# A state space block with its order on PE, DVE and ACT fixed by the program text, and its preparation cut into more steps

## The chip, the cores and the metric

The kernel runs on one core of one Trainium2 chip. Its time is device microseconds for one execution, as the median of several runs. A profile of one further execution gives every instruction with its engine, its start and its length. The engines are named as the profile names them: PE (TensorE's matmuls), PEld (its weight loads), DVE (VectorE), ACT (ScalarE), POOL (GpSimd) and SP (SyncE, which issues the DMAs here).

## The reference

Two layers, each of an attention-like block and a feed-forward block with residuals: attention, a mixture of 32 experts with top 8, a state space block, and a gated feed-forward whose weights are looked up in a table of 16 values. All arrays are f32; there are 2 sequences of 1024 tokens, and the model's width is 512. The change lies in the third block and in the beginning of the fourth:

```python
def _L1_attn_ref(x, w_in, w_param, w_out):        # 16 heads, D_STATE = D_HEAD = CHUNK = 64
    xr = x @ w_in.T
    inp, res = (xr[..., :D_INNER], xr[..., D_INNER:])
    params = (x @ w_param.T).reshape(b, l, N_HEADS, PARAM_DIM)
    dt = jax.nn.softplus(params[..., 0])
    a = jnp.exp(-dt)
    Bp = params[..., 1:1 + D_STATE]
    Cp = params[..., 1 + D_STATE:]
    y = _ssd(a.reshape(nb, l), ...)                # heads and tokens reshaped flat: nb = b * heads
    out = y.reshape(b, l, D_INNER) * jax.nn.silu(res)
    return out @ w_out.T

def _ssd(a, Bm, Cm, X, Q):
    cs = jnp.cumsum(jnp.log(a).reshape(nb, nc, Q), axis=-1)
    L = jnp.where(tri, jnp.exp(cs[..., :, None] - cs[..., None, :]), 0.0)
    y_diag = einsum('znij,znjh->znih', einsum('znid,znjd->znij', Cc, Bc) * L, Xc)
    states = einsum('znj,znjd,znjh->zndh', jnp.exp(cs[..., -1:] - cs), Bc, Xc)
    # scan over chunks: S = exp(cs[..., -1]) * S + states
    y_inter = einsum('znid,zndh,zni->znih', Cc, S_prev, jnp.exp(cs))
    return (y_diag + y_inter).reshape(nb, l, dh)

x = x + _L1_attn_ref(_layernorm(x), ...)
x = x + _L1_ffn_ref(_layernorm(x), ...)            # h = silu(gate(x)) * up(x); down(h)
```

## The kernel before

The kernel computes the four blocks in turn. For the attention and the expert blocks the order of the instructions on PE, DVE and ACT is that of the program text (`tc.manual_schedule`); SP's and POOL's order is a planner's. For the state space block (`_state_space`) and the final feed-forward (`_FeedForward`) a planner, which has priorities from the program's order and its own estimate of each instruction's time, orders all engines ahead of the launch. On the chip each engine then takes its instructions strictly in that order, and waits where an operand or a buffer isn't ready.

The state space block takes 128 tokens of each of the two sequences at a time: a stage `st`, eight in all. Each stage has eight chunks `c`, and `k = 8 st + c` counts them.

- `prepare(st)` loads the residual rows `x` and the experts' sums `part`, adds them (L1370) and takes their moments (L1372, L1373), the root and the reciprocal (L1375, L1376); normalises and turns the rows (L1381, L1387, L1388); multiplies by the step weights (`dt`, L1393), sends `dt` through HBM into another layout (L1400, L1403), takes the softplus by Exp and Ln (L1410, L1411), and sums it with a triangular matrix (`la`, `laT`, `cs`: L1423 to L1431); the sums go to HBM as `cs_rows` (L1433). It is a generator, with four `yield`s.
- `features(st)` makes B, C, X and the gate for a stage: 32 groups of matmuls into one of two PSUM banks (`pf`, L1443). A group of the first 24 is copied out by four copies, ACT and DVE in turn (L1460, L1462); a group of the last eight (the gate) by one copy (L1469 or L1471). Every group ends with a `yield`.
- `begin(k)` loads the rows `csb` by two DMAs (L1484), turns B and X for the chunk (`bx`, L1489 to L1492), makes the decays (`dec`, L1495 on DVE, Exp at L1499 on ACT), `xd` and `cd` on POOL, and `ec` (Exp, L1513).
- `weights(k)` multiplies C by B (`cb`, L1529) and by the decay (`wgt`, L1535). `products(k)` makes the state (L1547, L1579), the output (`ps_y`, L1557, L1569), and multiplies it into the gate (L1592).
- `project_out(st)` multiplies a stage's output by `wout` (`so`, L1598), adds it to `x` (L1603) and stores it in `x3` (L1605), in two halves.

The main loop (L1619) interleaves them: while stage `st` runs its chunks, the features of `st + 1`, the output of `st - 1` and the preparation of `st + 2` are given out between them by `step`. In the last stage there are no features; the final feed-forward's first tokens are normalised and its first units run there (`_FeedForward.begin`, L1698; `unit`, L1681). PSUM's eight banks are two for features (`ps_f`), two for turns and projections (`ps_t`), and one each for `st`, `y`, `cb0` and `cb1`.

Ahead of the loop two preparations and the features of stage 0 are written one after the other:

```python
        for st in range(2):
            for _ in prepare(st):
                pass
        for _ in features(0):
            pass
        begun = begin(0)
        wgt = weights(0, begun[1])
```

## Time and profile before

Three runs took 2804.3, 2810.66 and 2813.29 us; the median is 2810.66. The profiled execution took 2820.1 us, of which 2818.4 lie between its first and last instruction.

| | PE | PEld | DVE | ACT | POOL |
|---|---|---|---|---|---|
| busy in the whole span, us | 2703.1 | 1624.1 | 1425.4 | 933.1 | 635.7 |
| share | 96% | 58% | 51% | 33% | 23% |

The mean granted TensorE clock is 0.982 of full speed. The state space block runs from about 1550 us to 2403 us: the loads of its first rows wait for the experts' last scattered sums until 1556 us, its first matmul runs at 1566.8, the Silu of the gate, which opens a stage, runs at 1646.96, 1730.91, 1827.97, 1925.09, 2022.16, 2119.21, 2216.39 and 2307.49, and the last output projection ends at 2396.5. Of DVE's 50.1 us in a middle stage (1825.9 to 1923.0), 15.8 copy features out, 10.3 make the decays and 9.2 the gate products. In the block the loads are light: the DMA engines are busy for a sixth of the time in a middle stage.

A line of a profile view shows the source line, the engine, the operation, the tile written and the tiles read (out<-in), shapes and counts. In the order of time a line begins with start and length in us, and ends in brackets with the idle time of the engine before it and who ended it. In the table by stretches, each line has its borders and length, and then the busy time of each engine with its number of instructions, the granted clock, the share of the DMA engines and GB/s.

### The profile page before, as it was taken

What the parts mean: (1) busy time and instruction counts of PE and PEld (TensorE: products, weight loads), DVE (VectorE), ACT (ScalarE), POOL (GpSimd) and SP (SyncE); (2) the same over time, 40 slices, a digit from 0 to 9 for tenths busy, and PEclk for the clock granted to TensorE, in tenths of its full rate; (3) what the DMA queues carried; (4) which work ended last, traced back from release to release, by engine and by line L of the source; (5) the groups of instructions that cost most, each with busy time, mean ns of one, the idle gap of its engine ahead of it and who ended that gap; (6) DMA issues with size and microseconds to landing.
All of it is one profiled execution on the core that took longest, in us unless ns stands there. A gap on an engine that the chain in (4) does not pass through costs nothing. (4 is left out here: it accounts for less than half of the span.)

```text
span 2818.4 us, 34644 instructions
## 1 busy us (share of the span) xinstructions
PE 2703.1 (96%) x11976; PEld 1624.1 (58%) x11976; DVE 1425.4 (51%) x3952; ACT 933.1 (33%) x1887; POOL 635.7 (23%) x787
## 2 busy tenths in 40 slices
PE   7999999998989899999999699999999999999999
PEld 3444444544465566666665587777777775444444
DVE  5555543655236788987775344554455453101100
ACT  1344432443323233333333333443444433101010
POOL 2222220433355634333333000110111010000000
PEclk9999999998989999999999799999999999999999
DMA  3376532212479999998886301111111140100000
GB/s 115 111 199 184 164 115 70 92 60 74 153 247 248 241 228 255 263 240 202 205 205 107 84 16 36 38 41 44 28 47 42 35 147 20 34 8 27 30 0 26
DMA packets 242793, 315.60 MB, mean 112 GB/s; under 512 B 60753, under 2 KB 129361, under 8 KB 241841
## 3 DMA queue, kind: packets, MB, share of 16 engines
q1 hardware_dynamic: 208320, 234.87, 28.0%
q0 software_dynamic: 33280, 77.68, 13.1%
q8 instruction: 98, 1.61, 0.2%
q10 hardware_dynamic: 1008, 0.73, 0.1%
q14 instruction: 87, 0.70, 0.1%
HBM read 160.17 MB, written 153.04 MB: 111 GB/s over the span
## 5 line engine op out<-in xcount | busy, mean ns | idle before, releaser
L1080 PE MATMUL pg<-xgT,wgu 128*128 128x256 f32 (+1 forms) x1536 | 447.2, 444 | 13.8 <-DVE hT L1093 12.7
L1080 PEld LDWEIGHTS pg<-xgT,wgu 128*128 128x128 f32 x1536 | 289.0, 194 | 161.1 <-issue 51.2
L1142 POOL DMA_INDIRECT acc<-y,tok x160 | 272.9, 1706 | 401.8 <-ACT y L1140 186.7
L943 DVE SCALAR_TENSOR_TENSOR acc<-hit,lut,acc 128x688 f32<-128x688 bf16 (+2 forms) x405 | 348.8, 861 | 14.4
L1443 PE MATMUL pf<-xT,win 128*128 128x256 f32 x1024 | 242.5, 385 | 5.5 <-ACT gate L1471 3.8
L653 ACT ACTIVATE pT<-st 128x512 f32<-128x512 f32 (+3 forms) x384 | 158.7, 497 | 180.6 <-PE st L640 158.0
L548 PE MATMUL sp<-ka,qa 64*128 64x512 f32 (+3 forms) x768 | 207.3, 511 | 8.1 <-DVE mx L569 4.0
L1443 PEld LDWEIGHTS pf<-xT,win 128*128 128x128 f32 x1024 | 187.0, 190 | 38.8 <-PE pf L1443 7.2
L640 PE MATMUL st<-qa,ka 64*128 64x512 f32 (+3 forms) x768 | 182.4, 512 | 2.3 <-issue 1.5
L569 DVE TENSOR_REDUCE mx<-sp 128x1 f32<-128x384 f32 (+3 forms) x352 | 167.3, 492 | 17.4 <-PE sp L548 10.7
L657 POOL TENSOR_SCALAR_AFFINE_SELECT pT<-pT 128x128 f32<-128x128 f32 x256 | 83.5, 338 | 390.2 <-ACT pT L653 378.3
L296 POOL DMA_INDIRECT rows<-row,idx x128 | 128.7, 1005 | 108.3 <-DVE chosen L282 43.6
L1750 PE MATMUL po<-wd,f_hT 128*128 128x512 f32 (+1 forms) x352 | 152.6, 592 | 0.0
L671 PE MATMUL y<-pT,v 128*64 128x512 f32 (+3 forms) x768 | 145.7, 512 | 4.6 <-ACT raw L608 3.1
L562 DVE CUSTOM_DVE_ANT_0 junk<-sp,cmask 128x128 f32<-128x128 f32 x256 | 73.3, 286 | 145.3 <-PE sp L548 135.4
L548 PEld LDWEIGHTS sp<-ka,qa 64*128 64x128 f32 x768 | 91.8, 187 | 93.5 <-issue 49.7
L1694 DVE TENSOR_TENSOR f_hT<-s,pu 128x512 f32<-128x512 f32 (+1 forms) x37 | 25.5, 688 | 232.8 <-PE pu L1688 232.8
L640 PEld LDWEIGHTS st<-qa,ka 64*128 64x128 f32 x768 | 102.3, 192 | 63.2 <-issue 36.9
L1515 POOL TENSOR_TENSOR cd<-ft_c,ec 128x256 f32<-128x256 f32 x56 | 40.8, 730 | 413.3 <-PE cb L1529 205.2
L1140 ACT ACTIVATE y<-yo,rw 128x512 f32<-128x512 f32 x128 | 81.2, 684 | 157.9 <-PE yo L1133 150.1
L1443 PE MATMUL pf<-xT,wc 128*128 128x256 f32 x512 | 125.0, 391 | 8.8 <-DVE ft_b L1462 5.2
L1688 PE MATMUL pg<-f_xT,wg 128*128 128x512 f32 (+1 forms) x296 | 133.4, 593 | 0.0
(213 smaller groups left out, 4034.3 us busy)
## 6 DMA issues: line engine op xcount, KB each, us to landing
rows<-blank SPq DMA_DIRECT2D x160, 272.5 KB
xg<-rows SPq DMA_DIRECT2D x32, 817.5 KB
xg<-rows SPq DMA_DIRECT2D x32, 545.0 KB
csb<-cs_rows SPq DMA_DIRECT2D x128, 128.0 KB
wgu<-in_wg_dram SPq DMA_DIRECT2D x32, 256.0 KB
wgu<-in_wu_dram SPq DMA_DIRECT2D x32, 256.0 KB
wd<-in_wd_dram SPq DMA_DIRECT2D x32, 256.0 KB
wd<-in_wd_dram SPq DMA_DIRECT2D x64, 128.0 KB
```

Of the source, the lines that this page charges most:

```text
L296: t = tc.nc.gpsimd.indirect_dma_start(out=self.rows[:, :], out_offset=bass.IndirectOffsetOnAxis(ap=idx[:, i, k : k + 1], axis=0), in_=xr[i ...
L548: nc.tensor.matmul(sp[hh][:, c0:c1], lhsT=q[half, pr, tb * P : (tb + 1) * P], rhs=k[half, pr, k0 * P : k1 * P], start=True, stop=True,)
L569: nc.vector.tensor_reduce(m[:, n : n + 1], sp[hh][:, c0:c1], AX.X, ALU.max)
L640: nc.tensor.matmul(st[:, c0:], lhsT=k[half, j // 2, kb * P : (kb + 1) * P], rhs=q[half, j // 2, qt * 512 + c0 : (qt + 1) * 512], start=Tru ...
L653: e = nc.scalar.activation(pT[:, c0:], st[:, c0:], AF.Exp)
L671: nc.tensor.matmul(y[j // 2][half, c0:], lhsT=v[:, kb, h // 2, h % 2 : h % 2 + 2, :].rearrange("p k d -> p (k d)"), rhs=ps[j][:, c0:], sta ...
L943: nc.vector.scalar_tensor_tensor(acc, hit, lut[:n, k : k + 1], acc, ALU.mult, ALU.add)
L1080: nc.tensor.matmul(pg, lhsT=wgu[:, cc, m * P : (m + 1) * P], rhs=xgT[:, cc, :cols], start=cc == 0, stop=cc == NCC - 1,)
L1142: nc.gpsimd.indirect_dma_start(out=self.router.acc[to][:, :], out_offset=bass.IndirectOffsetOnAxis(ap=tok[:, j : j + 1], axis=0), in_=y, i ...
L1443: nc.tensor.matmul(pf, lhsT=w[wn][:, cc, c0 : c0 + P], rhs=xT[st][:, cc], start=cc == 0, stop=cc == NCC - 1,)
L1688: nc.tensor.matmul(dst[:n, :], lhsT=w[:, cc, fc * P : fc * P + n], rhs=self.xT[tt][:, cc, :], start=cc == 0, stop=cc == NCC - 1,)
L1750: nc.tensor.matmul(po, lhsT=self.hT[tt][fc // 4][:n, fc % 4, j * P : (j + 1) * P], rhs=wd[:n, fc, :], start=fc == 0, stop=fc == NFC - 1,)
```

## The change

The whole of `_state_space` now runs under `tc.manual_schedule` for PE, DVE and ACT: these three take their instructions in the order in which the text gives them out. SP and POOL stay with the planner.

- `prepare` has seven `yield`s where it had four: after its loads, between the moments of its two blocks of rows, and after `dt`'s way through HBM. It begins in chunk 3 (loads), goes on in chunk 4 (two steps: a sum and its moments each, the second with root and reciprocal), chunk 5 (normalise and turn), 6 (`dt`) and 7 (softplus), and its last step (`laT`, `cs`) comes at the start of chunk 2 of the following stage. It was given out in chunks 4 to 7.
- The loads of `csb` are taken out of `begin` and given out by `load` a chunk earlier. `begin` becomes a generator of two parts, and feature groups are given out singly, between them.
- In chunk 0 of each stage, where ACT has the Silu of the gate, all four copies of a feature group go to DVE (`busy`).
- Ahead of the loop, steps of the two preparations are written between the groups of features(0).
- In the last stage the feed-forward's rows are both loaded at once, into two tiles, its moments are taken in a second step and all four blocks turned in a third; a unit is given out in two halves. At the end, units that were begun are finished.

```diff
@@ -1354,7 +1354,9 @@
         def block(st, b):
             return (b * T + st * ST) // P
 
-        xs, xT, cs_rows, csT, gate, ft = {}, {}, {}, {}, {}, {}
+        xs, xT, cs_rows, csT, gate, ft, csbs = {}, {}, {}, {}, {}, {}, {}
+
+        busy = [False]
 
         def prepare(st):
 
@@ -1365,12 +1367,13 @@
                 r = slice(block(st, b) * P, (block(st, b) + 1) * P)
                 nc.sync.dma_start(out=x[:, b, :], in_=acc[0][r, :])
                 nc.sync.dma_start(out=part[:, b, :], in_=acc[1][r, :])
+            yield
             mv = g["small"].tile([P, B, 2], F32, tag="ln_mv", name="ln_mv")
             for b in range(B):
                 nc.vector.tensor_tensor(x[:, b, :], x[:, b, :], part[:, b, :], ALU.add)
-                stats = g["small"].tile([P, 6], F32, tag="ln_st", name="ln_st")
-                nc.vector.bn_stats(stats, x[:, b, :])
-                nc.vector.bn_aggr(mv[:, b, :], stats)
+                _moments(nc, g, x, b, mv[:, b, :])
+                if b == 0:
+                    yield
             rstd = g["small"].tile([P, B], F32, tag="ln_rs", name="ln_rs")
             nc.scalar.activation(rstd, mv[:, :, 1], AF.Sqrt, bias=g["eps"])
             nc.vector.reciprocal(rstd, rstd)
@@ -1403,6 +1406,7 @@
             nc.sync.dma_start(
                 out=d, in_=dt_rows.rearrange("b (n t) h -> (b n) (t h)", t=CT)
             )
+            yield
 
             neg = wk.tile([NROW, P], F32, tag="neg", name="neg", bufs=1)
             nc.vector.tensor_scalar(neg, d, -1.0, None, ALU.mult)
@@ -1456,7 +1460,7 @@
                             src = pf[h2 * HB : (h2 + 1) * HB, b, :].rearrange(
                                 "p (c t) -> p c t", t=CT
                             )
-                            if h2 == 0:
+                            if h2 == 0 and not busy[0]:
                                 nc.scalar.copy(dst, src)
                             else:
                                 nc.vector.tensor_copy(dst, src)
@@ -1475,15 +1479,22 @@
 
             return [(s, b, b * SCH + s * NCH + c) for s in range(NSEQ) for b in range(B)]
 
+        def load(k):
+
+            if k < NST * NCH:
+                st, c = divmod(k, NCH)
+                csb = csbs[k] = wk.tile([P, NSEQ, B, P], F32, tag="csb", name="csb", bufs=3)
+                for s in range(NSEQ):
+                    nc.sync.dma_start(
+                        out=csb[:, s], in_=cs_rows[st][:, s, c, :].partition_broadcast(P)
+                    )
+
         def begin(k):
+
 
             st, c = divmod(k, NCH)
             f = ft[st]
-            csb = wk.tile([P, NSEQ, B, P], F32, tag="csb", name="csb", bufs=3)
-            for s in range(NSEQ):
-                nc.sync.dma_start(
-                    out=csb[:, s], in_=cs_rows[st][:, s, c, :].partition_broadcast(P)
-                )
+            csb = csbs.pop(k)
             pt = ps_t.tile([P, 2, NSEQ, P], F32, tag="t", name="bx_ps")
             for s in range(NSEQ):
                 nc.tensor.transpose(pt[:, 0, s, :], f["b"][:, s * NCH + c, :], g["ident"])
@@ -1497,6 +1508,7 @@
                     ALU.subtract, ALU.min,
                 )
             nc.scalar.activation(dec, dec, AF.Exp)
+            yield
             xd = cd = ec = None
             if c < NCH - 1:
 
@@ -1513,7 +1525,9 @@
                     nc.scalar.activation(ec[half], csb[half, :, b, :], AF.Exp)
                 cd = wk.tile([P, NSEQ, P], F32, tag="cd", name="cd")
                 nc.gpsimd.tensor_tensor(cd, f["c"][:, c :: NCH, :], ec, ALU.mult)
-            return bx, dec, xd, cd, ec
+            made[k] = bx, dec, xd, cd, ec
+
+        made = {}
 
         def weights(k, dec):
 
@@ -1609,44 +1623,63 @@
             for _ in range(n):
                 next(it, None)
 
-        for st in range(2):
-            for _ in prepare(st):
-                pass
-        for _ in features(0):
+
+        first, second, feats = prepare(0), prepare(1), features(0)
+        for of, n in ((first, 1), (second, 1), (first, 3), (feats, 4), (first, 1), (feats, 3),
+                      (second, 1), (feats, 2), (second, 1), (feats, 1), (first, 1), (feats, 4),
+                      (first, 1), (second, 1), (feats, 4), (second, 1), (feats, 5), (second, 1),
+                      (feats, 4), (second, 1), (feats, 6)):
+            step(of, n)
+        load(0)
+        load(1)
+        for _ in begin(0):
             pass
-        begun = begin(0)
-        wgt = weights(0, begun[1])
+        wgt = weights(0, made[0][1])
+        ahead = iter(())
         for st in range(NST):
             lasts = iter(())
             if st == NST - 1:
                 last.weights = then()
                 last.banks = [(ps_f, "f"), (ps_f, "f")]
-                lasts = last.begin(wk, ps_t)
-            nc.scalar.activation(gate[st], gate[st], AF.Silu)
+                lasts = last.begin(wk, xp, ps_t)
             feats = features(st + 1) if st + 1 < NST else iter(())
             out = project_out(st - 1) if st else iter(())
-            ahead = prepare(st + 2) if st + 2 < NST else iter(())
             for c in range(NCH):
                 k = st * NCH + c
                 more = k + 1 < NST * NCH
-                if c < NCH - 1:
-                    nxt = begin(k + 1)
+                nxt = begin(k + 1) if more else iter(())
+                load(k + 2)
+                busy[0] = c == 0
+                if c == 0:
+                    nc.scalar.activation(gate[st], gate[st], AF.Silu)
+                if c == 2:
+                    step(ahead)
+                    ahead = prepare(st + 2) if st + 2 < NST else iter(())
+                if c == 3:
+                    step(ahead)
+                step(feats)
+                if c in (4, 5, 6):
+                    step(ahead)
+                step(nxt)
+                step(lasts, (1, 1, 2, 2, 1, 1, 1, 1)[c])
+                step(feats)
+                step(nxt)
                 if c < 2:
                     step(out)
-                step(lasts, (1, 0, 2, 2, 1, 1, 1, 1)[c])
-                step(feats, 2)
-                if c >= 4:
+                if c in (4, 7):
                     step(ahead)
                 step(feats)
-                if c == NCH - 1 and more:
-                    nxt = begin(k + 1)
-                bx, dec, xd, cd, ec = begun
+                bx, dec, xd, cd, ec = made.pop(k)
                 products(k, bx, xd, cd, ec, wgt)
                 if more:
-                    wgt = weights(k + 1, nxt[1])
-                    begun = nxt
+                    wgt = weights(k + 1, made[k + 1][1])
+                if c > 2:
+                    step(lasts)
                 step(feats)
+                busy[0] = False
         for _ in project_out(NST - 1):
+            step(lasts, 2)
+        while last.begun > last.done:
             step(lasts)
 
 
@@ -1657,6 +1690,7 @@
     def __init__(self, tc, g, x3, out, big):
         self.tc, self.g, self.x3, self.out, self.big = tc, g, x3, out, big
         self.hT, self.xT = {}, {}
+        self.begun = self.done = 0
 
     def rows(self, fc):
         return FTAIL if fc == NFC - 1 else P
@@ -1679,11 +1713,15 @@
         ]
 
     def unit(self, tt, fc, pool, tag):
+
         nc = self.tc.nc
         wg, wu, _ = self.weights
         n = self.rows(fc)
+        self.begun = fc + 1
         p = [q.tile([P, TT], F32, tag=k, name="p" + k) for q, k in self.banks]
-        for dst, w in zip(p, (wg, wu)):
+        for i, (dst, w) in enumerate(zip(p, (wg, wu))):
+            if i:
+                yield
             for cc in range(NCC):
                 nc.tensor.matmul(
                     dst[:n, :], lhsT=w[:, cc, fc * P : fc * P + n], rhs=self.xT[tt][:, cc, :],
@@ -1695,25 +1733,28 @@
             self.hT[tt][fc // 4][:n, fc % 4, :], s[:n, :], p[1][:n, :], ALU.mult
         )
 
-    def begin(self, wk, psum):
+    def begin(self, wk, xp, psum):
 
         nc, g = self.tc.nc, self.g
+        x = [
+            wk.tile([P, B, D], F32, tag="part", name="part", bufs=1),
+            xp.tile([P, B, D], F32, tag="x", name="x", bufs=3),
+        ]
         for i in range(2):
-            x = wk.tile([P, B, D], F32, tag="part", name="part", bufs=1)
-            self.load(x, self.tokens(0)[2 * i : 2 * i + 2])
-            norms = _norms(nc, g, x, range(B))
-            yield
-            if i == 0:
-                self.room(0)
-            nc.vector.reciprocal(norms[1], norms[1])
+            self.load(x[i], self.tokens(0)[2 * i : 2 * i + 2])
+        yield
+        norms = [_norms(nc, g, x[i], range(B)) for i in range(2)]
+        yield
+        self.room(0)
+        for i in range(2):
+            nc.vector.reciprocal(norms[i][1], norms[i][1])
             for b in range(B):
-                xn = _normed(nc, x, b, b, norms, wk, ("xn", D))
+                xn = _normed(nc, x[i], b, b, norms[i], wk, ("xn", D))
                 _turn(nc, g, xn, 2 * i + b, self.xT[0], psum, "t")
             yield
-        self.done = 0
         for fc in range(NFC):
+            yield from self.unit(0, fc, wk, "xn")
             self.done = fc + 1
-            self.unit(0, fc, wk, "xn")
             yield
 
     def rest(self):
@@ -1760,7 +1801,8 @@
             pending = None
             for tt in range(NTT):
                 for fc in range(0 if tt else self.done, NFC):
-                    self.unit(tt, fc, wk, "s")
+                    for _ in self.unit(tt, fc, wk, "s"):
+                        pass
                 if pending is not None:
                     down(*pending)
                 pending = (tt, x)
@@ -1868,7 +1910,10 @@
 
     big = second.enter_context(tc.tile_pool(name="ss_big", bufs=2, reuse_waits="tile"))
     last = _FeedForward(tc, g, x3, out, big)
-    _state_space(tc, g, a, w, acc, x3, last_weights, big, last)
+    with tc.manual_schedule(
+        engines={getattr(mybir.EngineType, n) for n in ("PE", "DVE", "Activation")}
+    ):
+        _state_space(tc, g, a, w, acc, x3, last_weights, big, last)
     last.rest()
     second.close()
 ```

## The prediction

> **What bounds the kernel now.** I read the page's slices first: PE is at nine tenths or more almost everywhere, so the block that changes can only give back the time in which PE stands or runs at half clock. Next the busy time by stretch, cut at the block's own borders (time, PE, PE's weight loads, DVE, ACT, POOL busy, then granted clock):
>
> ```profile
> 1547.80:1566.80 19.00, 0.56 (x6) 0.18 (x3) 4.14 (x10) 3.42 (x5) 4.66 (x3) 0.62 0.78 177
> 1566.80:1646.10 79.30, 72.58 (x331) 61.34 (x332) 29.55 (x97) 27.96 (x75) 1.80 (x4) 0.90 0.14 36
> 1825.90:1923.00 97.10, 95.09 (x592) 71.66 (x591) 50.09 (x165) 40.51 (x94) 10.65 (x21) 1.00 0.16 39
> 2214.30:2305.30 91.00, 90.78 (x562) 68.86 (x561) 44.49 (x148) 33.41 (x85) 10.50 (x21) 1.00 0.16 44
> 2305.30:2403.40 98.10, 98.10 (x451) 49.44 (x450) 32.71 (x94) 31.58 (x44) 8.90 (x17) 1.00 0.30 108
> ```
>
> In order: the wait for the scattered sums (the change doesn't touch it), the start (prepare(0), prepare(1), features(0)), one middle stage, the stage without a prepare, the last stage. PE is the bound of every one but the first; DVE is half busy. PE's busy time hides short waits, since each matmul's modelled end lies 0.16 us behind the next start, so I took starts from the order of time. Sixteen feature groups in a row show the undisturbed rate; then a chunk that waits:
>
> ```profile
> 1616.80 27.79 PE L1443 MATMUL pf<-xT,win 128*128 128x256 f32 x128
> ...
> 1868.60 1.89 PE L1443 MATMUL pf<-xT,wc 128*128 128x256 f32 x8
> 1871.13 1.97 PE L1443 MATMUL pf<-xT,wc 128*128 128x256 f32 x8 [0.63 <-DVE ft_c L1462]
> 1873.35 1.97 PE L1443 MATMUL pf<-xT,wc 128*128 128x256 f32 x8 [0.26 <-DVE ft_c L1462]
> 1875.24 0.45 PE L1547 MATMUL ps_st<-xd,bx 128*64 128x64 f32 x8
> ```
>
> A group costs 27.6/16 = 1.73 us. The waits are for the feature banks: there are two, and a group's four copies out go ACT, DVE, ACT, DVE, each behind the one before:
>
> ```profile
> 2248.61 0.26 ACT L1460 COPY ft_c<-pf 64x128 f32<-64x128 f32 x1
> ...
> 2248.90 0.29 DVE L1462 COPY ft_c<-pf 64x128 f32<-64x128 f32 x1 [0.47 <-ACT ft_c L1460]
> 2249.22 0.26 ACT L1460 COPY ft_c<-pf 64x128 f32<-64x128 f32 x1 [0.36 <-DVE ft_c L1462]
> 2249.51 0.29 DVE L1462 COPY ft_c<-pf 64x128 f32<-64x128 f32 x1 [0.32 <-ACT ft_c L1460]
> ```
>
> That is 1.2 us when both engines are free, and longer by whatever either engine has ahead of a copy.
>
> A middle stage lasts 97.1 us (first output projections start at 1728.81, 1825.87, 1922.99, 2020.06, 2117.11, 2214.29). By starts its work is: 32 groups 55.2; eight chunks of 0.44 (transposes) + 0.28 + 0.54 + 0.58 + 0.65, less 0.9 in the first and last, 19.0; a 0.1 us pause after each cb, 0.8; output projection 2 x 6.87 = 13.7; prepare 0.9 + 1.7 + 0.9 = 3.5. Sum 92.2. So about 4.9 us per stage are waits: that is what a better order can win.
>
> **The change, part by part.** No matmul and no element of work is added. The order on PE, DVE and ACT becomes that of the program text, so I walked the text, each engine strictly in order, with these durations (busy time over count, in a middle stage): DVE copy 0.29, dec 0.30, gate 0.29, wgt 0.38, state 0.24, add and bn_stats 0.67 each, aggregate 0.18, xn 0.5; ACT copy 0.26, bx 0.59, dec 0.63, ec 0.42, table load 1.28; 0.2 us from a matmul's issue end to its reader, 0.03 to 0.06 for other hand-overs. I count t from a chunk's start on PE.
>
> *Chunks 0, 1, 3, 6, 7.* Copies end before their bank is due: 0 to 0.4 us of waits each; I take 0. In chunks 0 and 1 the output projection (6.87 us on PE) covers everything, also that chunk 0's copies all go to DVE (16 more of 0.29, less than the projection), and the 3.2 us of Silu with its table. The chunk's csb loads a chunk ahead cost PE nothing; today DVE waits for csb 0.5 us in all of a stage, so they win nothing either. SP issues the same DMAs: what is queued behind prepare's (issued now in chunk 3) are csb rows due a chunk later.
>
> *Chunk 2: prepare's last step* is put ahead of the first group. PE transposes la (0.25), then cs needs laT, and DVE still has the last chunk's state, gates, wgt and the last group's copies (2 x 0.29 with waits for ACT) ahead of it. Walked: PE stands 1.4 us. Today that wait is filled by a feature group. +1.4.
>
> *Chunk 4* gives DVE two adds with moments, 2 x 1.52, on top of 2.3 (copies) + 1.2 + 0.5 + 1.2 + 0.8 = 6.0, and it stands for the square root (ACT's table load, 1.28): from 9.5 to 10.1. Copies slip: group 3 leaves its bank at t = 11.3 instead of 6.4, and group 1 of chunk 5 starts at 11.4 instead of 9.7. +1.7 and +0.3.
>
> *Chunk 5: prepare's turn* stands right behind that group. PE is free at 13.1, but DVE must first finish wgt (13.8), the copies of two groups (15.7) and xn (16.2): the transpose starts at 16.3. +3.2, and 0.3 for the transposes' bank. Even with no backlog from chunk 4 it waits for its own group's copies (1.4) and xn (0.6): 2.1 at least. Everything behind it, bx, dec, products, moves with it.
>
> Sum of a middle stage: 92.2 + 1.4 + 2.0 + 3.5 = 99.1 against 97.1: +2.0, five times, +10.0. With durations taken as means of single instructions (dec 0.35, for example, where overlap isn't taken off) the walk gives +2.7. Stage 0 (no cs step, but the start's backlog): 85.5 against 83.9 between Silus, +1.5. Stage 6 has only the cs step: 91.2 against 91.1, 0.
>
> *Last stage.* PE has no wait today (98.10 of 98.10). The norms now fall into chunk 1, the four turned blocks into chunk 2, all in one step: xn, transpose, copy, four times through two banks behind dec, while PE has nothing but them. Walked: 4.6 us of waits there, 1.5 for the first unit's bank; an eighth unit done here is one fewer behind. +6.
>
> *Start.* Today it pays for idle time and a second stretch at half clock; by the new order features run behind the first turn at once, but Exp and Ln with their two table loads (3.2 us) stand ahead of ACT copies, twice (4.4 us of waits over four groups, and 2.2), cs and the second turn wait 1.4 each. Walked end of features(0): 1643.5, against 1644.4, and PE then goes on with fewer breaks: -2.
>
> Waits together: +10.0 + 1.5 + 0 + 6 - 2 = +15.5.
>
> *Half clock* is a cost that this trace shows once inside the block:
>
> ```profile
> 1593.29:1596.70 3.41, 1.83 (x10) 1.31 (x9) 2.95 (x11) 2.81 (x7) 0.00 (x0) 1.00 0.58 125
> 1596.70:1600.12 3.42, 1.25 (x6) 0.69 (x4) 0.65 (x2) 3.36 (x6) 0.00 (x0) 1.00 0.46 111
> 1600.12:1603.53 3.41, 2.44 (x7) 1.43 (x8) 1.15 (x5) 1.41 (x5) 0.00 (x0) 0.50 0.07 22
> 1603.53:1606.95 3.42, 3.42 (x9) 2.70 (x9) 0.59 (x3) 0.42 (x2) 0.00 (x0) 0.50 0.02 5
> ```
>
> A stretch of 3.4 us with 1.83 of PE busy kept the clock, the next with 1.25 lost it, for 6.8 us (about 3.4 us of work lost). Chunk 5's turn leaves 1.7 + 3.2 us of waits within 7 us, so a stretch of 3.4 can hold anything from 0.2 to 1.7 of work: on either side of those two rows, by where it falls. There are seven such places (stages 0 to 5, and the last stage's 4.6): 0 to 7 x 3.4 = 24. I take three of seven, +10, because the stretches' phase is not mine to choose.
>
> [...]
>
> **Forecast.** +15.5 + 10 = +25.5 on the profiled execution's 2820.1 (span 2818.4 and 1.7 around it), 2845.6. That execution lies 9.4 above the median of the runs, 2810.66; the difference carried over gives 2836. Its own range: waits from +6 (chunk 5 at 2.1, no backlog) to +21 (single means), clock 0 to +24: 2817 to 2856.
>
> **Rivals.**
> (1) *It does what it is written for*: the waits go. 4.9 x 5 in the middle stages, about 2 each in stages 0 and 6, and some 5 of the start: up to -33. For it: DVE is only half busy, and every copy's own chain (1.2 us plus 0.2) is shorter than a group. Against: the turn's transposes directly behind the xn they need. A half of it, -16, gives 2795.
> (2) *The chains are shorter than I walk and it comes out even*: chunk 5 at 2.1, chunk 4 at 0, no half clock: a stage is 95.7, -1.4 x 5, against +4 in the last stage and -2 at the start: -5, 2806.
> (3) *Half clock every time*: 15.5 + 24 = +39.5, 2850. It decides from the point where chunk 5's two waits together leave under some 1.3 us of work in a 3.4 us stretch.
>
> **Chances.** My forecast, waits with some half clock: 0.45. Rival 3: 0.2. Rival 2: 0.15. Rival 1: 0.2. 0.3% (8.4 us) is about what these runs can tell from no change. Faster by more: rival 1, 0.20. Within: rival 2 with the lowest of the forecast's own range, 0.16. Slower: 0.64. The likeliest's own range is 2817 to 2856; to leave no more than two in ten out it must reach to rival 2 and the milder part of rival 1: 2800 to 2855.
>
> **What would show it.** In the changed profile: first, an idle time of 2 to 3.5 us on PE before the first xn transpose of each stage, put down to DVE xn, and DVE busy without break for the 10 us ahead of it. Second, 1.4 us before cs, put down to laT. Third, granted clock at 0.5 for 6.8 us behind some of the turns. Fourth, a last stage of some 104 us where 98.1 stood. I am wrong if the middle stages are 95 us or less, that is, if PE's transposes find xn done; or if the copies out of a group no longer pass from ACT to DVE and back.

## The result, and the profile after

The changed kernel took 2830.2 us (median of six runs, 2826.69 to 2839.86), the kernel before 2811.34 beside it (six runs, 2804.3 to 2815.4): a ratio of 1.0073, with a 95% interval of 1.0061 to 1.0086. It is slower by some 20 us (18.9 by the medians, 20.5 by the ratio).

Its profiled execution took 2833.87 us, span 2832.0: 13.6 us more than the span before. All of it is in the block that was changed. From the first xn transpose to the first down-projection of the second block of tokens in the feed-forward, the time went from 961.9 us (1566.8 to 2528.69) to 985.9 (1556.42 to 2542.32), +24.0. What runs ahead of it, which nothing touched, was 10.4 us shorter in this execution. Split at the first output projection of each stage:

| part | before | after | difference |
|---|---|---|---|
| start, to the first feature group of stage 0's loop | 79.3 | 79.7 | +0.4 |
| stage 0 | | | +1.4 |
| five middle stages | 485.5 | 504.05 | +18.6 |
| stage 6 | | | +1.0 |
| last stage and what follows it | 223.35 | 226.0 | +2.7 |

The changed text puts two feature groups (3.5 us) ahead of a stage's first output projection. So stage 0 went from 82.7 to 87.6 us and stage 6 from 91.0 to 88.5, and the table gives both with these groups taken off and added back. In the same way 0.5 us of transposes moved from the start into stage 0: up to the end of features(0) the start is +0.9, and stage 0 is then +0.9 too.

The table by stretches, as it was shown of before (PE, weight loads, DVE, ACT, POOL busy, granted clock, DMA share, GB/s): the start, two middle stages, the last stage.

```profile
1556.40:1636.10 79.70, 70.49 (x327) 59.47 (x327) 24.27 (x81) 23.07 (x66) 0.00 (x0) 0.92 0.08 21
1825.00:1924.60 99.60, 93.97 (x591) 72.08 (x590) 52.07 (x173) 36.50 (x86) 10.37 (x21) 1.00 0.15 38
1924.60:2025.90 101.30, 95.66 (x591) 73.28 (x590) 52.00 (x173) 36.64 (x87) 10.37 (x21) 0.98 0.14 38
2316.30:2420.00 103.70, 101.16 (x458) 51.07 (x457) 37.51 (x113) 39.59 (x55) 9.73 (x19) 0.98 0.31 107
```

A middle stage was 97.1 us with 95.09 of PE busy. It is now 99.6 with *less* PE time, 93.97: 5.63 us of PE's time are open waits, where 2.0 stood. The next line is the stage that follows, with a granted clock of 0.98: its PE time is 1.69 longer for the same 591 matmuls. What PE waited for over the block (total us, times, longest), first two lines of the kernel before, then the changed one:

```profile
PE xn_ps L1387 <- DVE xn L1381: 18.4, 1, 18.4
PE cs_ps L1427 <- DVE laT L1425: 0.3, 1, 0.3
```

```profile
PE xn_ps L1390 <- DVE xn L1384: 37.0, 8, 19.3
PE pf L1447 <- DVE ft_x L1466: 10.6, 7, 3.0
PE cs_ps L1431 <- DVE laT L1429: 9.7, 8, 1.3
PE pf L1447 <- DVE ft_c L1466: 2.6, 2, 2.2
PE ln_pt L95 <- DVE ln_xn L85: 2.5, 1, 2.5
```

The 19.3 is the wait for the first rows, which is the 18.4 of before. Before, no stage waited for xn, and one wait for laT, of 0.3, is all that shows. In order of time, one middle stage's four waits (start, length, and in brackets the idle time and who ended it):

```profile
1954.71 0.41 PE L1431 MATMUL cs_ps<-tri,laT 128*32 128x128 f32 x2 [1.34 <-DVE laT L1429]
...
1985.60 1.97 PE L1447 MATMUL pf<-xT,win 128*128 128x256 f32 x8 [1.27 <-DVE ft_x L1466]
1990.36 1.11 PE L1390 MATMUL xn_ps<-ident,xn 128*128 128x128 f32 x8 [2.80 <-DVE xn L1384]
1991.69 0.33 PE L1500 MATMUL bx_ps<-ident,ft_b 128*128 128x128 f32 x1 [0.22 <-ACT xT L1391]
```

1.34 + 1.27 + 2.80 + 0.22 = 5.63: these four are all of it, and they stand at the places that the prediction named. The cause of the 2.80 is read from DVE in the same microseconds:

```profile
1985.48 0.47 DVE L1593 SCALAR_TENSOR_TENSOR state<-state,ec,ps_st 128x64 f32<-128x64 f32 x2
1985.87 1.19 DVE L1606 TENSOR_TENSOR gate<-ps_y,gate 64x128 f32<-64x128 f32 x4
1987.09 0.76 DVE L1549 TENSOR_TENSOR wgt<-cb,dec 128x256 f32<-128x256 f32 x2
1987.88 0.29 DVE L1466 COPY ft_x<-pf 64x128 f32<-64x128 f32 x1
1988.49 0.62 DVE L1466 COPY ft_x<-pf 64x128 f32<-64x128 f32 x2 [0.32 <-ACT ft_x L1464]
1989.43 0.29 DVE L1466 COPY ft_x<-pf 64x128 f32<-64x128 f32 x1 [0.32 <-ACT ft_x L1464]
1989.76 1.00 DVE L1384 TENSOR_SCALAR xn<-x,ln_mv,ln_rs 128x512 f32<-128x512 f32 x2
```

xn's last operand, the reciprocal of the root, was ready at 1984.56. It runs at 1989.76 because the text puts it behind a chunk's gates, weights and the copies of a group, two of which stand still for ACT. PE stands for the last 2.80 us of it. The half clock that follows, in stretches of 3.41 us (columns as above):

```profile
1985.37:1988.79 3.42, 1.97 (x8) 1.44 (x8) 2.96 (x11) 0.55 (x3) 0.00 (x0) 1.00 0.61 193
1988.79:1992.21 3.42, 1.63 (x13) 1.35 (x14) 2.64 (x8) 1.33 (x3) 0.00 (x0) 1.00 0.04 17
1992.21:1995.62 3.41, 3.41 (x11) 2.70 (x10) 0.00 (x0) 2.50 (x3) 0.49 (x2) 0.50 0.02 5
1995.62:1999.03 3.41, 3.41 (x35) 2.58 (x35) 1.41 (x6) 1.86 (x6) 1.00 (x2) 1.00 0.03 8
```

One stretch of 3.4 us at 0.50 with PE busy throughout, and then full speed. It happened behind four of the six turns (the transposes of xn, one in each of stages 0 to 5), once in the last stage, and for 6.8 us in the start (as before).

### The profile page after: what moved, and what is told of

Read it like the earlier page. It is cut to its first block, busy times and chain, and to the rows that moved or that the text cites. A ratio compares the mean times of both kernels' runs of the same rounds, so it can differ in the third digit from the quotient of the medians.

```text
span 2832.0 us, 34744 instructions
## 1 busy us (share of the span) xinstructions
PE 2694.0 (95%) x11976; PEld 1628.7 (58%) x11976; DVE 1437.5 (51%) x4008; ACT 909.0 (32%) x1827; POOL 631.4 (22%) x787
## 4 chain that ended last, share of the span: by engine, by line
PE 89%; DVE 5%; DMA 2%; ACT 2%; issue 1%; SPq 0%; ACTq 0%; DVEq 0%; POOLq 0%
PE pg L1080 15%; PE pf L1447 15%; PE sp L548 5%; PE po L1791 5%; PE st L640 5%; PE y L671 4%; PE pg L1726 4%; PE pu L1726 4%; PE pq L487 4%; PE so L1612 4%; PE yo L1128 4%; PE xg_ps L1070 2%; PE yo L1133 2%; PE pv L462 2%; PE pf L1726 2%; PE po L686 2%
## 5 line engine op out<-in xcount | busy, mean ns | idle before, releaser
L1447 PE MATMUL pf<-xT,win 128*128 128x256 f32 x1024 | 240.7, 387 | 10.6 <-DVE ft_x L1466 10.6
L1447 PEld LDWEIGHTS pf<-xT,win 128*128 128x128 f32 x1024 | 192.7, 193 | 41.0 <-issue 13.3
L1517 POOL TENSOR_TENSOR xd<-bx,dec 128x128 f32<-128x128 f32 x112 | 42.8, 403 | 635.1 <-issue 281.0
L942 DVE TENSOR_SCALAR hit<-short 128x688 bf16<-128x688 bf16 (+2 forms) x405 | 130.2, 321 | 1.7
```

The source lines that it names most:

```text
L942: nc.vector.tensor_scalar(hit, short, float(k), None, ALU.is_equal)
L1447: nc.tensor.matmul(pf, lhsT=w[wn][:, cc, c0 : c0 + P], rhs=xT[st][:, cc], start=cc == 0, stop=cc == NCC - 1,)
```

## The experiments

The kernels ran in three groups of four, on chips where the kernel before took 2808.89, 2823.02 and 2826.09 us. So the ratios to it are compared, each with its 95% interval, and a ratio is turned into us by 2810.66. What runs ahead of the block differs by up to 18 us between the profiled executions, so where a trace is compared, its time runs from the first xn transpose to the end: +24.0 us in the changed kernel against the one before.

**First group: what is to blame?** One edit mends the turn, one takes the fixed order off, one puts the fixed order on the old text, one moves the moments.

*The turn apart.* The transposes become a step of their own; one feature group, chunk 5's second, stands between their xn and them:

```diff
+            xns = []
             for b in range(B):
                 xn = wk.tile([P, D], F32, tag="xn", name="xn")
+                xns.append(xn)
...
+            yield
+            for b, xn in enumerate(xns):
                 pt = ps_t.tile([P, NCC, P], F32, tag="t", name="xn_ps")
...
-                if c in (4, 7):
+                if c in (4, 5, 7):
                     step(ahead)
```

> The transposes of a prepare are given out two feature steps behind the xn that they read (xn on DVE at its old place in chunk 5, transposes ahead of the third group of chunk 5). Theory (PE waits in order for xn): the 2.8 us wait and the 0.2 us for the bank go in six stages, 18 us, and with them most of the four half-clock stretches of 3.4 us (1.65 us each): 15 to 24 us below the changed kernel's 2830, so 2806 to 2815. The 1.3 us ahead of chunk 5's first group stays. Rival (the loss is spread over DVE's whole queue, the turn is only where it shows): the wait comes back at the next group, and less than 6 us are won.

2816.19 us, 1.0024 [1.0012, 1.0037]: +7 us where the changed kernel has +20.5, so 14 us are won, just short of the 15 expected. A stage is 97.86, the wait for xn is gone from the stages and so is the half clock there. By the traces 17.2 us are won: 10.4 are waits (6 turns x 1.74, against a stage of 99.6 without half clock), and some 7 stand beside the stretches at half clock that are gone. But of the 3.0 us won at the turn 1.2 comes back: feature groups waited for their bank 19 times, not 7.

```profile
PE pf L1451 <- DVE ft_x L1470: 18.1, 19, 3.0
PE cs_ps L1435 <- DVE laT L1433: 9.7, 8, 1.3
```

DVE is as late as before; PE only meets it one group later (1.27 before chunk 5's first group, 0.94 before its second).

*The planner's order.* `_state_space` is called without `manual_schedule`; the text is the changed one to the last word:

```diff
-    with tc.manual_schedule(
-        engines={getattr(mybir.EngineType, n) for n in ("PE", "DVE", "Activation")}
-    ):
-        _state_space(tc, g, a, w, acc, x3, last_weights, big, last)
+    _state_space(tc, g, a, w, acc, x3, last_weights, big, last)
```

> The new text, with the order on all engines left to the planner again. Theory (the fixed order loses the time, the text's new cut doesn't): turns and cs move between features again, 2800 to 2820, no wait on xn over 0.5 us in a stage. Rival (the finer steps or the early loads themselves cost): 2825 or more.

2790.61 us, 0.9936 [0.992, 0.9953]: faster than both kernels, by 18 us against the one before and 38.5 against the changed one, and faster than was expected. A stage is 94.56. Its waits in the block (19.9 is the first rows'):

```profile
PE xn_ps L1390 <- DVE xn L1384: 19.9, 1, 19.9
PE pf L1447 <- DVE ft_c L1466: 5.2, 10, 1.2
PE pf L1447 <- DVE ft_x L1466: 2.1, 1, 2.1
PE la_ps L1427 <- DVE la L1422: 1.2, 1, 1.2
```

*The old text, fixed.* The kernel before, with the same `manual_schedule` around its call:

```diff
-    _state_space(tc, g, a, w, acc, x3, last_weights, big, last)
+    with tc.manual_schedule(
+        engines={getattr(mybir.EngineType, n) for n in ("PE", "DVE", "Activation")}
+    ):
+        _state_space(tc, g, a, w, acc, x3, last_weights, big, last)
```

> The old text, with its order on PE, DVE and ACT taken as it stands. Theory: far slower than the changed kernel, since whole steps of prepare stand between chunks: per stage the adds behind their own loads, the softplus behind dt's way through HBM (some 5 us of DVE standing, copies behind it) and the turn behind its xn, 10 to 20 us a stage, and some 25 us at the start: 2890 to 2980. Rival (how the steps are cut matters little once the order is fixed): within 15 us of 2830.

2928.91 us, 1.0432 [1.0415, 1.045]. A stage is 109 to 110, and from the start to stage 0's projection it takes 197 us where the kernel before takes 162. So the new text is worth 121 - 20.5 = 100 us *under a fixed order*, and still doesn't reach what the planner makes of either text.

*The moments a chunk earlier* (on top of the turn apart): loads in chunk 2, the two sums with moments in chunks 3 and 4.

```diff
                     ahead = prepare(st + 2) if st + 2 < NST else iter(())
+                    step(ahead)
...
-                if c in (4, 5, 7):
+                if c in (5, 7):
                     step(ahead)
```

> As the first of these, and the loads and the two moments of a prepare a chunk earlier each (loads in chunk 2, first block's moments in chunk 3, second's in chunk 4, each ahead of or behind the first group), so that chunk 4 has one set of them and not two. Theory: chunk 4's DVE backlog goes as well, 1.3 us more per stage, 6 to 9 us below the first of these: 2799 to 2808. Rival: chunk 5's first group waits as before for the copies, no change against the first.

2821.02 us, 1.0045 [1.0029, 1.0062]: not faster than without it, where the theory had it 6 to 9 us faster; it is some 5 us slower, with intervals that overlap. Stages are 98.07 (one, with half clock, 98.55) where they were 97.86. So the backlog wasn't the load of DVE alone. ACT loads a table for the square root and another for the Exp behind it:

```profile
1971.83 1.28 ACT L1378 ACT_TABLE_LOAD   x1
1973.85 0.29 ACT L1378 ACTIVATE ln_rs<-ln_mv,eps 128x2 f32<-128x2 f32 x1 [0.73 <-DVE ln_mv L67]
1974.05 0.57 ACT L1507 COPY bx<-bx_ps 128x512 f32<-128x512 f32 x1
1975.47 1.28 ACT L1514 ACT_TABLE_LOAD   x1 [0.86 <-DVE dec L1510]
1976.77 0.63 ACT L1514 ACTIVATE dec<-dec 128x512 f32<-128x512 f32 x1
1977.30 0.24 ACT L1468 COPY ft_x<-pf 64x128 f32<-64x128 f32 x1
1977.58 0.29 DVE L1470 COPY ft_x<-pf 64x128 f32<-64x128 f32 x1 [2.18 <-ACT ft_x L1468]
1978.63 1.69 PE L1451 MATMUL pf<-xT,win 128*128 128x256 f32 x4 [1.56 <-DVE ft_x L1470]
```

The copy at 1977.30 stands behind all of that on ACT; DVE's next copy waits 2.18 us for it, and PE 1.56 for the bank. Both loads, and a wait of 2.18 on DVE, were in the turn apart too, with the second load a chunk later (1886.89), where PE lost 0.31 us by it. The waits for banks only changed their places: 20.7 us in all in either kernel. That the place of the loads makes the difference is read from these lines; no run moved it alone.

**Second group: which engine's order?**

*PE alone fixed*, and in the next kernel *DVE and ACT fixed, PE free* (there the tuple is `("DVE", "Activation")`):

```diff
-        engines={getattr(mybir.EngineType, n) for n in ("PE", "DVE", "Activation")}
+        engines={getattr(mybir.EngineType, n) for n in ("PE",)}
```

> The changed text with its order on PE alone; DVE's and ACT's order is the planner's. PE's order is the changed kernel's to the instruction. Theory (PE stands because the copies, laT and xn lie behind prepare's other work in DVE's and ACT's queues): most of the waits go although PE's order is the same. What is left is what PE's own order costs: xn behind the copies of one group, 1 to 2 us a stage, cs some 0.6 us a stage. 2797 to 2812. Rival (PE's order is at fault: turn and cs stand directly behind what they read): at least the 2.8 us and the 1.3 us per stage stay, 2820 or more.

> The changed text with its order on DVE and ACT; PE's order is the planner's. DVE's and ACT's orders are the changed kernel's to the instruction. Theory: little is won, since the copies that free the feature banks leave as late as before: 2815 to 2830. Rival (PE's order is at fault): 2810 or less.

PE alone: 2809.16 us, 0.9959 [0.9941, 0.9977], stages of 95.15. PE's order is the changed kernel's, instruction by instruction, and yet the wait for xn is gone from every stage and the one for laT is 0.4 at most:

```profile
PE xn_ps L1390 <- DVE xn L1384: 19.1, 1, 19.1
PE pf L1447 <- DVE ft_c L1466: 3.7, 8, 1.6
PE cs_ps L1431 <- DVE laT L1429: 3.1, 8, 0.4
```

On DVE, the planner puts xn far ahead of the text's place: its second block runs at 1955.13, and the first transpose on PE is at 1976.61.

```profile
1954.80 0.41 DVE L1549 TENSOR_TENSOR wgt<-cb,dec 128x256 f32<-128x256 f32 x1
1955.13 0.77 DVE L1384 TENSOR_SCALAR xn<-x,ln_mv,ln_rs 128x512 f32<-128x512 f32 x1
1955.82 0.34 DVE L1506 SCALAR_TENSOR_TENSOR dec<-csb,csT,mask 128x128 f32<-128x128 f32 x1
```

DVE and ACT fixed: 2822.84 us, 1.0004 [0.9988, 1.002], stages of 96.76. With PE free, it takes a feature group and cb products ahead of the xn transposes, and the waits for xn and laT are gone too. By the ratio that is 1 us over the kernel before, between the theory (little is won) and its rival. Left is the bank that DVE's copies free late, and 95.48 us of PE time in a stage where the changed kernel has 93.97, which no run explains:

```profile
PE pf L1447 <- DVE ft_x L1466: 8.3, 7, 1.3
```

From the changed kernel's +20.5, freeing DVE and ACT gives back 32 us, freeing PE 19.5, freeing all 38.5. DVE and ACT were not freed one without the other.

*The turn and cs apart*, and *the best order by hand* that I found. The first adds to the turn apart a `yield` behind laT's copy, and gives cs out behind chunk 2's first group. The second also takes the last stage's xn a step ahead of their transposes, and in the start cuts the softplus behind its Ln, with seven feature groups around it (those that its list gives out in twos) copied by DVE alone:

```diff
             nc.vector.tensor_copy(laT, pt)
+            yield
...
                 step(feats)
+                if c == 2:
+                    step(ending)
...
             nc.scalar.activation(d, d, AF.Ln, bias=1.0)
+            yield
...
-            for b in range(B):
-                xn = _normed(nc, x[i], b, b, norms[i], wk, ("xn", D))
-                _turn(nc, g, xn, 2 * i + b, self.xT[0], psum, "t")
-            yield
+        xn = [_normed(nc, x[0], b, b, norms[0], wk, ("xn", D)) for b in range(B)]
+        yield
+        for b in range(B):
+            _turn(nc, g, xn[b], b, self.xT[0], psum, "t")
```

> The order fixed on all three; turn apart from xn as in the first experiment (2816 there), and cs a feature group behind laT. Theory: cs no longer waits 1.34 us in stages 1 to 6 and at the start: 8 to 10 us below the first experiment, 2805 to 2809. Rival (DVE's backlog comes out at the next bank): 2812 or more.

> The order fixed on all three, with every place taken apart that the profile named except chunk 4: turn and cs as in the kernel beside this; in the last stage xn ahead of its transposes by a step; at the start the softplus cut behind Ln, with the two groups behind it copied by DVE alone. Theory: another 2 to 3 us from the last stage's wait of 2.5, and 5 to 9 from the start's 2.2 and 3.0 and its half-clock stretch: 2793 to 2802, faster than the kernel before. Rival (waits move on): 2805 or more.

With cs apart: 2824.69 us, 1.0008 [0.9995, 1.0021], stages of 96.59. The 1.27 us per stage went as expected and the waits for banks didn't grow. The whole gave less than the 8 to 10 us expected: about 4.5 by the ratio (1.0024 to 1.0008), with intervals that overlap, and 6.8 by the traces, with a stretch at half clock in the last stage that the turn apart didn't have. The best by hand: 2816.49 us, 0.9974 [0.9957, 0.9992]: faster than the kernel before by 7 us, some 1 us short of the gain expected, with the same stages of 96.59 and 5.9 us less up to stage 0's projection (159.8 against 165.7). It stays behind the planner's 0.9936; the intervals only just miss each other.

**Third group: what of the text wins, under the planner?** Each takes one thing out of the faster kernel: the early csb loads (`load(k)` goes back into `begin`); the spread of prepare (chunks 4 to 7 again); the mixed start (the two preparations and the features one after the other); chunk 0's copies on DVE alone (`busy` stays False).

```diff
             f = ft[st]
+            load(k)
...
-                load(k + 2)
```

```diff
                 if c == 2:
-                    step(ahead)
                     ahead = prepare(st + 2) if st + 2 < NST else iter(())
-                if c == 3:
-                    step(ahead)
                 step(feats)
-                if c in (4, 5, 6):
-                    step(ahead)
...
-                if c in (4, 7):
-                    step(ahead)
+                if c >= 4:
+                    step(ahead, (3, 1, 2, 1)[c - 4])
```

```diff
-        for of, n in ((first, 1), (second, 1), (first, 3), (feats, 4), (first, 1), (feats, 3),
...
-            step(of, n)
+        for of in (first, second, feats):
+            for _ in of:
+                pass
```

```diff
-                busy[0] = c == 0
+                busy[0] = False
```

> The changed text under the planner (0.9936 of the kernel before in the second experiment), with the csb loads back in begin, where the kernel before has them. Theory: DVE waited for csb 0.5 us in all of a stage before, so the early loads won little: 0.993 to 0.995 of the kernel before. Rival (the loads ahead are the gain): 0.997 or more.

> The changed text under the planner, with prepare given out where the kernel before has it: loads, both moments and root in chunk 4 behind the second group, turn in 5, dt and softplus in 6, cs in 7. Theory (preparation spread over more chunks is the gain: the planner takes its priorities from the text, and before it put both moments and the turn into chunks 2 and 3, with 0.6 to 0.8 us waits for banks): the middle stages go back from 94.6 to 96 to 97, 0.997 to 1.000 of the kernel before. Rival (single feature groups between begin's halves are the gain): stays at 0.993 to 0.995.

> The changed text under the planner, with both preparations and features(0) written one after the other ahead of the loop, as before. Theory: the planner mixes them by itself, but with prepare(1) ahead of all features: 2 to 5 us at the start, 0.9945 to 0.9955. Rival (the hand-mixed start is most of the gain): 0.997 or more.

> The changed text under the planner, with chunk 0's copies shared by ACT and DVE again. Theory: chunk 0 has the output projection's 6.9 us of PE over it, so nothing changes: 0.992 to 0.995. Rival (ACT's Silu holds up the copies, and DVE alone relieves it): 0.997 or more.

| taken out | us | ratio | 95% | change against 0.9936 | change in the trace |
|---|---|---|---|---|---|
| nothing | 2790.61 | 0.9936 | 0.992 to 0.9953 | | |
| early csb loads | 2804.62 | 0.9938 | 0.9919 to 0.9957 | +0.5 us | +0.5 us |
| spread of prepare | 2818.98 | 0.9985 | 0.997 to 1.0 | +14 us | +12.8 us |
| mixed start | 2812.83 | 0.9968 | 0.9952 to 0.9985 | +9 us | +4.9 us |
| copies on DVE | 2807.02 | 0.994 | 0.9916 to 0.9963 | +1 us | +3.6 us |

The loads and the copies move nothing that these runs can tell (of the copies' 3.6 us in the trace, 3.2 lie ahead of stage 0's projection). The spread of prepare is the largest part; without it the stages go back to 96.3 to 98.3, and the banks are late again:

```profile
PE pf L1447 <- DVE ft_c L1466: 11.8, 10, 1.9
```

The start is between the two figures expected, and its interval overlaps that of the whole: 161.5 us to stage 0's projection against 157.1, or 4 us, and that profile has two separate drops of the clock in the start. By the ratios the parts of 14 and 9 sum to more than the whole of 18, and their intervals overlap. By the traces they are 12.8 and 4.9 of 19.3, which fits, and 11.6 of the 12.8 lie in the five middle stages. Each trace is one execution.

## Why the prediction held

It said slower, at 2836 within 2800 to 2855; it was 2830.2. The mechanism was the one forecast, on PE a wait for xn, laT and banks that DVE frees late; its terms came out so:

| step | forecast | measured |
|---|---|---|
| cs in chunk 2, per stage | 1.4 | 1.34 |
| bank before chunk 5's first group | 1.7 | 1.27 |
| xn at the turn, and the transposes' bank | 3.2 and 0.3 | 2.80 and 0.22 |
| a middle stage without half clock | 99.1 | 99.6 |
| stage 0, stage 6 | +1.5, 0 | +1.4, +1.0 |
| start | -2 | +0.4 |
| last stage | +6 | +2.7, with 0.9 of clock in it |
| half clock | 3 of 7 places, 3.4 each, +10 | 5 of 7, 0.9 to 1.65 each, +7 |

*The whole came out closer than its parts, and that is luck.* In the block +24.0 was measured against the forecast's +25.5: some 17 of waits where 15.5 was forecast, and 7 of half clock where 10 was. Of the waits, the last stage was put some 4 too high, the five middle stages 2.6 too low, the start 2.4 and stage 6 1.0 too low.

*The stage's sum is right by two errors that cancel.* Its waits are 5.63, not 6.9, and its work is 99.60 - 5.63 = 94.0, not 92.2. The second is the one with a consequence: 92.2 made 4.9 us per stage look like waits that an order could win. The planner's own best here, 94.56 with 0.65 of waits, gives the same work of some 93.9, so 3.2 per stage were there to win, and 2.5 of them were won.

*Half clock.* The trace of before had shown one drop of 6.8 us, and I priced every place by it. A drop behind a turn lasts 3.4 us and costs 1.65 in three stages (101.3 against 99.6) and 1.0 in one (100.6); the one in the last stage costs 0.9 against the turn apart, which has the same last stage without a drop. It came more often than I took. "On either side of those two rows, by where it falls" was right: the drops start at 1790.82, 1992.21, 2091.20, 2193.60 and 2336.95, all whole multiples of 3.413 us apart. The six turns have the same waits (2.80 before the transposes), and two kept the clock; that where this grid cut them made the difference is my estimate, and no run shows it.

*Last stage.* The wait is there, 2.54 before the first of 16 transposes, and is the one open wait; I had walked 4.6, and 1.5 for the first unit's bank. The clock drops at 2336.95, half a microsecond ahead of the transposes, and they take 0.9 us longer than in the turn apart. 2.54 + 0.9 is 3.4 where +2.7 was measured; where 0.7 came back wasn't tried.

*Start.* The waits walked for the groups behind the softplus (4.4 over four groups, then 2.2) were there: 2.17 and 3.01 are the longest. The gain that I set against them was too high, so the start is 2.4 above its forecast.

*The signs.* PE's wait before the transposes and the 1.3 before cs are as described. DVE wasn't busy without break: in the 10 us ahead of that turn it worked 7.0, and stood for ACT's copies in most of the rest. Half clock lasted 3.4 us, not 6.8. The last stage of 103.7 has the sign's number, but part of it is work that moved there; against a common end it is +2.7.

*The rivals.* Rival 1, "it does what it is written for", is wrong for this kernel and right for its text: without the fixed order it gives -18, near the -16 that I gave it by halving; the half was a guess. What the forecast lacked lies here. I had taken the order as the one thing the change could win or lose by; it is two things. The text spreads prepare over six chunks and mixes the start, worth 18 us by a planner's hand, and the fixed order costs 38.5 us on top of that text. The forecast saw the difference of the two only. And "even with no backlog from chunk 4 it waits for its own group's copies and xn: 2.1 at least" holds for DVE and ACT in the text's order alone: with PE's order kept and theirs free, that wait was 0. Rival 2 is out by the turn's 2.80 where it had 2.1 and by the half clock. Rival 3 was near in count, five of seven, and had the price at twice what it was; its 1.3 us was an estimate from the one row that fell, with 1.25, and here a drop came behind a stretch with 1.63.

*Nothings that were nothing.* The csb loads and the copies of chunk 0 were put at 0, and both runs say 0 within their intervals. Those runs are under the planner; under the fixed order neither was tried.

## What to carry to other kernels

Where three engines have their order fixed by one text, look for a DVE instruction that the text puts right ahead of its reader on PE. Here xn was one: it ran behind a chunk's gates, weights and copies on DVE, and PE waited 2.80 us a stage for it. Give a helper engine's work out some groups ahead of its reader, or leave that engine to a planner that does. A text that is cut into finer steps and the fixing of its order are two changes, to be measured apart: here one wins 18 us and the other loses 38.5. And a PE time per stage, from which waits are counted, was known here to no better than 1 to 2 us in 94: the sum of starts gave 92.2, and a stage's length less its open waits 95.1 in the kernel before but 94.0 in the changed one and 93.9 under the planner.

## What the hardware showed that I had not expected

*PE's busy time doesn't part the drops.* In the changed kernel's trace the five drops named above, and the one of 6.8 us in the start, at 1592.85, lie on one grid of 3.413 us. Over it, the stretch ahead of a drop held 1.06, 1.11, 1.11, 1.36 and 1.63 us of PE's busy time (and 1.92 in the start), while 1.55 and 1.74 in the two turns that were spared kept the clock. There is no bound in this busy time, in which the ends of matmuls are modelled, that parts these. What does part them was not shown.

*A drop with PE busy throughout.* With DVE and ACT fixed and PE free, one stage fell to half clock with PE busy throughout (columns as above), and was 98.45 us long where the others took 96.76:

```profile
2086.20:2089.62 3.42, 3.42 (x23) 2.83 (x21) 0.68 (x3) 2.51 (x4) 0.00 (x0) 1.00 0.02 5
2089.62:2093.04 3.42, 3.42 (x30) 3.03 (x30) 0.88 (x3) 2.63 (x8) 1.34 (x3) 1.00 0.00 0
2093.04:2096.45 3.41, 3.41 (x11) 2.69 (x10) 2.58 (x9) 0.19 (x1) 0.15 (x1) 0.50 0.60 55
```

In the second of these stretches PE was busy for 3.42 of 3.42 us, and the third ran at 0.50: in this execution a busy PE didn't keep the clock. By its place in the stage before, where they start at 1993.96 and take 1.96 us, the 16 matmuls of `dt`, with 16 columns each, lie in the second stretch; that is an estimate from one stage's length of 96.76. No run changed these small matmuls, so what made the clock drop here was not shown.
